# Mean convolutions of a graph network on Trainium2: column halves of the array for alternate tiles, and another spread of a side computation over the two convolutions

## The chip, the core and the metric

The kernel runs on one core of a Trainium2 chip. The core has a matrix engine (TensorE, PE in the profile, with its weight loads shown as PEld), a vector engine (VectorE, DVE), a scalar engine (ScalarE, ACT), a gather and custom engine (GpSimd, POOL) and a queue engine that issues transfers (SyncE, SP). They run side by side, each in its own order, and wait for one another by semaphores. On-chip memory (SBUF) has 128 partitions; products land in the accumulators (PSUM), 128 partitions too.

The metric is the device time of one execution in microseconds (us), less is better. It takes in the whole network, of which the change touches one stage.

## The reference

The network has 3125 nodes with 64 features and 100000 edges, sorted by destination. Four blocks stand one after the other, each on h = max(layernorm(x), 0), and each adds its result to x: a stack of three transformer convolutions, a tensor-field convolution, two mean convolutions, and two relational convolutions over 65 edge types. The change is in the third block:

```
def _sage_conv(x, src, dst, n_nodes, w_l, b, w_r):
    msg = x[src]
    agg = segment_sum(msg, dst, num_segments=n_nodes)
    cnt = segment_sum(ones, dst, num_segments=n_nodes)
    mean = agg / maximum(cnt, 1.0)[:, None]
    return mean @ w_l + b + x @ w_r
...
h = relu(_sage_conv(x, src, dst, n, w1_l, b1, w1_r))
return _sage_conv(h, src, dst, n, w2_l, b2, w2_r)
```

The fourth block needs for each edge one over the number of edges of the same destination and the same relation (the mean inside each relation):

```
seg = dst * r + edge_type
cnt = segment_sum(ones, seg, num_segments=n * r)
mean = agg / maximum(cnt, 1.0)
```

Nothing in this count depends on the features, so the kernel does it beside the mean convolutions.

## The kernel before

**Nodes and adjacency.** Nodes lie on 125 partitions in 25 tiles (NP = 125, NT = 25, D = 64). Earlier, the kernel builds a dense table of edge counts between nodes in DRAM, `adj`; the sum over neighbours is then a product of the features with that table. One tile of the table, `adjr`, has 125 source nodes against all 3136 padded destinations (1568 KB in f32); its pool `sa` has four buffers.

**A mean convolution**, `sage(l, sp, fp, pp, beside)`, lines L1315 to L1353. It loads the weights `wl` and the bias `bb`. It holds seven accumulators `acc`, each of 64 partitions (features) by 448 destinations, and for each of the 25 tiles multiplies the tile's features into all seven (L1328): 175 products, each an f32 matmul, which the trace shows as two records. After that come the nodes' own terms: h is transposed in groups of four tiles (L168 on PE, the copy L169 on ACT, result `hT`), multiplied by the second weight in five groups of five (L1334, accumulator `pn`, which shares its place with the transposes), and the bias is added on DVE (L1335, `own`). The sums are copied to `agg` (L1338, four copies on DVE and three on ACT), multiplied by the first weight (L1342, 25 matmuls in five groups), divided by the count (L1345), added to `own` (L1347), and become the new h (L1349) in the first convolution. In the second they are added to x (L1351), with a layer norm behind (L152 to L160).

**The count beside it**, the generator `relation_counts`, L1045 to L1126, is advanced by `next(beside, None)` in the loop over tiles. Its steps:

1. A setup on DVE of some ten operations (L1052 to L1060).
2. 33 steps for pairs of relations, all on 128x784 f32: a mask (L1068), a forward scan (L1070), a backward scan (L1072) and a predicated copy (L1073) on DVE, and two small copies on ACT (L1074, L1075).
3. A middle section (L1079 to L1107). It sums what crosses partitions with four small matmuls on PE (L1086, L1087, from `rsums`, L1083) and prepares places and corrections on DVE.
4. 22 steps of three units each, 66 in all: a mask (L1112) on DVE, a scaled copy on ACT (L1114, two buffers `ract`), a predicated copy on DVE (L1115).
5. A closing part (L1119 to L1126), which ends with two operations on `wrel`: an addition (L1125) and a reciprocal (L1126).

```
for s in range(NT):
    for _ in range(2 if s % 3 else 1):
        next(beside, None)
    rows = sp.tile([P, AC], F32, name="adjr")
    after_added(dma(rows, adj.rearrange("(p t c) o -> p t (c o)", t=NT, c=AC)[:, s, :]).ins)
    for c in range(ANC):
        PE.matmul(acc[c], lhsT=h[:, s, :], rhs=rows[:NP, c * AW:(c + 1) * AW], start=(s == 0), stop=(s == NT - 1))
```

With this rule a convolution advances the count by 41 steps: the first takes the setup, all 33 pairs, the middle section and 6 of the 22 steps; the second takes the rest in its first ten tiles.

**What sets the order.** The kernel is written as one program; a planner in the framework then orders each engine's instructions by its own costs and dependences. Only the masks L1068 and L1112 are held to program order among themselves. So an instruction can stand on its engine well before or after its place in the source. All transfers named here are issued by SP, in that queue's order.

**Behind the stage** the relational block begins (`Relations`): weights `wr` are loaded, h is copied twice (`hh`, L1387 on DVE, L1388 on ACT), transposed, and multiplied by the relation weights (L1396, in two row halves), copied to `xs` (L1400) and stored. Its sums use `wrel`.

Of the kernel before, what the change touches and what calls it, by code (L numbers as in the profile page):

```python
# [9 lines left out]
F32 = mybir.dt.float32  # L10
# [8 lines left out]
P = 128  # L19
N = 3125  # L20
NP = 125
NT = 25
D = 64
# [16 lines left out]
AC = 3136  # L40
ANC = 7
AW = AC // ANC
# [6 lines left out]
def gnn_stack(ctx: ExitStack, tc: tile.TileContext, a: dict, out: bass.AP):  # L49
    nc = tc.nc  # L50
    V, S, PE, GP = nc.vector, nc.scalar, nc.tensor, nc.gpsimd
# [12 lines left out]
    def dma(dst, src):  # L64
        return nc.sync.dma_start(dst, src)
# [7 lines left out]
    def bcast_rows(ap, parts):  # L73
        n = ap.shape[-1]
        return bass.AP(tensor=ap.tensor, offset=ap.offset, ap=[[0, parts], [1, n]])
# [51 lines left out]
    adj = dram.tile([AROWS * AC, 1], F32, name="adj")  # L127
# [6 lines left out]
    h = node.tile([NP, NT, D], F32, name="h")  # L134
# [12 lines left out]
    def layernorm_relu(lp, t0, t1):  # L147
        n = t1 - t0
        st = lp.tile([NP, 3, n], F32, name="lnst", bufs=2)
        cen = lp.tile([NP, n, D], F32, name="lncen", bufs=2)  # L150
        sq = lp.tile([NP, n, D], F32, name="lnsq", bufs=2)
        V.tensor_reduce(st[:, 0, :], x[:, t0:t1, :], axis=AX.X, op=ALU.add)  # L152
        V.tensor_scalar(st[:, 0, :], st[:, 0, :], 1.0 / D, None, op0=ALU.mult)
        V.tensor_sub(cen, x[:, t0:t1, :], st[:, 0, :].unsqueeze(2).to_broadcast([NP, n, D]))
        S.activation(sq, cen, AF.Square)
        V.tensor_reduce(st[:, 1, :], sq, axis=AX.X, op=ALU.add)
        S.activation(st[:, 2, :], st[:, 1, :], AF.Sqrt, bias=eps, scale=1.0 / D)
        V.reciprocal(st[:, 2, :], st[:, 2, :])
        V.tensor_mul(cen, cen, st[:, 2, :].unsqueeze(2).to_broadcast([NP, n, D]))
        V.tensor_scalar(h[:, t0:t1, :], cen, 0.0, None, op0=ALU.max)  # L160
# [333 lines left out]
    def transposed(pool, pp, src, w, name):  # L494

        t = pool.tile([w, NT, NP], F32, name=name)
        transposed_tiles(pp, t, src, w, 0, NT)
        return t
# [361 lines left out]
    def after_each(ins, those, class_, reason):  # L860
        for st in those:
            tc.add_manual_dep(ins, st.name, mybir.DependencyInfo(class_, mybir.DependencyReason.DATA), reason=reason)

    def after_added(ins):
        after_each(ins, added, mybir.DependencyClass.Sync, "sums into the same places")
# [159 lines left out]
    with tc.tile_pool(name="fl", bufs=1) as fp, tc.tile_pool(name="flp", bufs=1, space=PSUM) as pp:  # L1025
# [7 lines left out]
        ps = pp.tile([1, 1], F32, name="ps")  # L1033
# [279 lines left out]


    def sage(l, sp, fp, pp, beside):  # L1315
        wl = fp.tile([D, 2, D], F32, name="wl")
        bb = fp.tile([NP, D], F32, name="bb")
        dma(wl[:, 0, :], a[f"L2_gnn_w{l}_l"])
        dma(wl[:, 1, :], a[f"L2_gnn_w{l}_r"])
        dma(bb, bcast_rows(a[f"L2_gnn_b{l}"], NP))  # L1320
        acc = [pp.tile([D, AW], F32, name=f"acc{c}") for c in range(ANC)]
        for s in range(NT):
            for _ in range(2 if s % 3 else 1):
                next(beside, None)
            rows = sp.tile([P, AC], F32, name="adjr")
            after_added(dma(rows, adj.rearrange("(p t c) o -> p t (c o)", t=NT, c=AC)[:, s, :]).ins)
            for c in range(ANC):
                PE.matmul(acc[c], lhsT=h[:, s, :], rhs=rows[:NP, c * AW:(c + 1) * AW], start=(s == 0), stop=(s == NT - 1))  # L1328
        own = fp.tile([NP, NT, D], F32, name="own")
        hT = transposed(fp, pp, h, D, "hT")  # L1330
        for t0 in range(0, NT, 5):
            ps = pp.tile([NP, 5, D], F32, name="pn", tag="ptr")
            for i in range(5):
                PE.matmul(ps[:, i, :], lhsT=hT[:, t0 + i, :], rhs=wl[:, 1, :], start=True, stop=True)  # L1334
            V.tensor_add(own[:, t0:t0 + 5, :], ps, bb.unsqueeze(1).to_broadcast([NP, 5, D]))  # L1335
        agg = fp.tile([D, AC], F32, name="agg")
        for c in range(ANC):
            (S.copy if c % 2 else V.tensor_copy)(agg[:, c * AW:(c + 1) * AW], acc[c])  # L1338
        for c, t0 in enumerate(range(0, NT, 5)):
            ps = pp.tile([NP, 5, D], F32, name=f"acc{c}")  # L1340
            for i in range(5):
                PE.matmul(ps[:, i, :], lhsT=agg[:, t0 + i:N:NT], rhs=wl[:, 0, :], start=True, stop=True)  # L1342
            o = own[:, t0:t0 + 5, :]
            m = fp.tile([NP, 5, D], F32, name="mean", bufs=2)
            V.tensor_mul(m, ps, rcnt[:, t0:t0 + 5].unsqueeze(2).to_broadcast([NP, 5, D]))  # L1345
            ht = h[:, t0:t0 + 5, :]
            V.tensor_add(m, o, m)  # L1347
            if l == 1:
                V.tensor_scalar(ht, m, 0.0, None, op0=ALU.max)  # L1349
            else:  # L1350
                V.tensor_add(x[:, t0:t0 + 5, :], x[:, t0:t0 + 5, :], m)  # L1351
                layernorm_relu(fp, t0, t0 + 5)

    with tc.tile_pool(name="rc", bufs=1) as rc, tc.tile_pool(name="sa", bufs=4) as sa, tc.tile_pool(
        name="sg", bufs=1
    ) as sg, tc.tile_pool(name="sgp", bufs=1, space=PSUM) as sgp:
        counting = relation_counts(rc, rc, sgp)
        sage(1, sa, sg, sgp, counting)
        sage(2, sa, sg, sgp, counting)
        for _ in counting:  # L1360
            pass
# [111 lines left out]
```

## Time and profile before

| | us |
|---|---|
| runs | 9271.43, 9261.91, 9268.46; median 9268.46 |
| profiled execution: its own time | 9271.42 |
| profiled execution: span on the profile | 9269.6 |
| the stage of the change, first count operation to first `hh` copy | 6367.4 to 6788.9 (421.5) |
| last h of the first convolution (L1349) ends | 6623.2 |
| products of the second convolution (L1328) end | 6742.2 |
| busy in 6367 to 6789: DVE, PE, ACT | 340.3, 328.7, 94.7 |

The page gives for each engine its busy time over the span. Since the blocks have different limits, the stage is read by itself. A timeline row of PE gathers neighbouring records of one kind: start, the time from the first start to the last end, and their number. A waits row names the waiting instruction and line, what released it, the total, how often, and the longest. In a tile's row stand the duration's minimum, median and maximum in ns and the first and last start in us.

### The profile page before, as it was taken

The numbers are of one execution on the slowest core, as the hardware profiler recorded it, in microseconds if no ns is written. First come the engines' busy times: TensorE is split into PE (matmuls) and PEld (weight loads), VectorE is DVE, ScalarE is ACT, GpSimd is POOL, SyncE is SP. The second block draws the span as 40 slices with busy tenths as digits, with TensorE's granted clock in tenths as the row PEclk, the third lists the DMA queues.
The fourth block names the chain that finished last, engine by engine and source line by source line (L and its number), as shares of the span: only waits on it lengthen the run. The fifth ranks groups of instructions, "written<-read, shape, count | busy, mean of one in ns | idle before, by whom it ended". The sixth has DMA issues, their size and how long they took to land. (4 is left out here: it accounts for less than half of the span.)

```text
span 9269.6 us, 70976 instructions
## 1 busy us (share of the span) xinstructions
PE 4731.1 (51%) x20300; PEld 3046.4 (33%) x20300; DVE 5564.9 (60%) x14292; ACT 992.4 (11%) x2654; POOL 6373.5 (69%) x5765
## 2 busy tenths in 40 slices
PE   5555545556455554888788788886770000320000
PEld 3333333333233333555555555552340000110000
DVE  7777766877677774666666666667842222322222
ACT  1111111111111111000000000001320000110000
POOL 3777767777677776888888888881006777447776
PEclk8555555555555556888888888887785555665555
DMA  5665636555355553444444444445463221442221
GB/s 181 205 204 192 204 123 206 198 175 176 114 172 178 174 174 97 108 107 104 112 111 104 112 105 111 103 99 183 171 205 81 52 53 51 127 152 53 51 53 47
DMA packets 677528, 1211.18 MB, mean 131 GB/s; under 512 B 323106, under 2 KB 468024, under 8 KB 633241
## 3 DMA queue, kind: packets, MB, share of 16 engines
q1 hardware_dynamic: 399586, 938.00, 29.3%
q0 software_dynamic: 277536, 268.52, 14.7%
q8 instruction: 163, 2.67, 0.1%
q14 instruction: 243, 1.98, 0.1%
HBM read 670.19 MB, written 535.54 MB: 130 GB/s over the span
## 5 line engine op out<-in xcount | busy, mean ns | idle before, releaser
L68 POOL DMA_INDIRECT kvg<-kvtd,srci x2352 | 2375.1, 1010 | 718.1 <-issue 681.7
L68 POOL DMA_INDIRECT msg<-xw,msgi x1568 | 1502.3, 958 | 1320.9 <-DMA xw<-xs 652.8
L1236 PE MATMUL pa<-cc,zT 128*128 128x256 f32 x6272 | 1623.7, 416 | 0.0
L876 POOL DMA_INDIRECT adj<-adjv,adji x784 | 1247.9, 1592 | 255.2 <-issue 236.8
L1236 PEld LDWEIGHTS pa<-cc,zT 128*128 128x128 f32 x6272 | 1265.5, 207 | 295.8 <-issue 116.9
L68 POOL DMA_INDIRECT xg<-xtf,srci x784 | 928.5, 1184 | 238.9 <-issue 199.5
L674 PE MATMUL pv<-msg,prevm 128*128 128x64 f32 x4 | 1.4, 442 | 2032.1 <-DVE msg L669 2032.1
L1225 DVE TENSOR_TENSOR zT<-xT,pb 128x512 f32<-128x512 f32 x980 | 611.3, 681 | 686.3 <-PE pb L1222 500.2
L78 DVE SCALAR_TENSOR_TENSOR msg<-msg,wrel 128x1024 f32<-128x1024 f32 x98 | 120.1, 1225 | 1390.7 <-DMA msg<-xw,msgi 1390.7
L509 DVE SCALAR_TENSOR_TENSOR data<-data,same 128x66 f32<-128x66 f32 (+2 forms) x3136 | 933.9, 298 | 27.7 <-DVE srest L81 0.3
L932 PE MATMUL pe<-we,eaT 128*128 128x256 f32 x1176 | 557.9, 634 | 768.5 <-DVE kvg L934 708.2
L509 DVE SCALAR_TENSOR_TENSOR qg<-qg,same 128x64 f32<-128x64 f32 (+1 forms) x2940 | 864.9, 294 | 40.8 <-DMA qg<-qtd,dsti 11.4
L934 DVE TENSOR_TENSOR kvg<-kvg,pe 128x1024 f32<-128x1024 f32 x294 | 358.5, 1219 | 691.7 <-DMA kvg<-kvtd,srci 612.6
L674 PEld LDWEIGHTS pv<-msg,prevm 128*128 128x128 f32 x4 | 1.0, 312 | 2033.5 <-issue 1018.3
L932 PEld LDWEIGHTS pe<-we,eaT 128*128 128x128 f32 x1176 | 337.9, 312 | 942.3 <-DVE kvg L934 780.6
L845 DVE SCALAR_TENSOR_TENSOR atie<-pk,akey,amuch 128x512 f32<-128x512 f32 x784 | 579.5, 739 | 43.1 <-PE pk L840 42.7
L840 PE MATMUL pk<-aplace,adig 128*128 128x128 bf16 x2352 | 298.6, 303 | 570.1 <-DVE atie L845 554.3
L840 PEld LDWEIGHTS <-adig 128*128 128x128 bf16 x2352 | 224.2, 138 | 782.3 <-DVE atie L845 432.0
L669 DVE SCALAR_TENSOR_TENSOR msg<-msg,same 128x64 f32<-128x64 f32 x1566 | 446.3, 285 | 56.1
L1210 PE MATMUL px<-ident,xg 128*128 128x128 f32 x784 | 204.9, 346 | 516.9 <-DMA xg<-xtf,srci 491.7
L788 PE MATMUL pw<-w,hid 64*128 64x128 f32 x3136 | 435.5, 410 | 22.2 <-ACT hid L748 22.2
L788 PEld LDWEIGHTS pw<-w,hid 64*128 64x128 f32 x3136 | 366.0, 294 | 124.8 <-issue 79.5
(316 smaller groups left out, 6426.5 us busy)
## 6 DMA issues: line engine op xcount, KB each, us to landing
wt<-wo SPq DMA_DIRECT2D x98, 1024.0 KB
kvg<-wt SPq DMA_DIRECT2D x49, 2048.0 KB
xw<-xs SPq DMA_DIRECT2D x50, 1820.0 KB
adjr<-adj SPq DMA_DIRECT2D x50, 1568.0 KB
qg<-qx SPq DMA_DIRECT2D x144, 512.0 KB
cum_tf<-data SPq DMA_DIRECT2D x49, 1152.0 KB
cum_dt<-data SPq DMA_DIRECT2D x98, 544.0 KB
qxf<-zeros SPq DMA_DIRECT2D x98, 512.0 KB
```

The costliest lines, as they stand in the source:

```text
L68: return GP.indirect_dma_start(out=dst, out_offset=None, in_=table, in_offset=bass.IndirectOffsetOnAxis(ap=idx, axis=0),)
L509: V.scalar_tensor_tensor(t[:, j], t[:, j - 1], same[:, s:s + 1], t[:, j], op0=ALU.mult, op1=ALU.add)
L669: V.scalar_tensor_tensor(m[:, j, :], prev, same[:, g * G + j:g * G + j + 1], m[:, j, :], op0=ALU.mult, op1=ALU.add)
L788: PE.matmul(pw[m][:, i, k, :], lhsT=hid[r, k, i0 + i, :], rhs=w2[r, :], start=False, stop=(i == 1 and k == 1))
L840: PE.matmul(ps[:, i, :], lhsT=dig[:, k, 4 * q + i:4 * q + i + 1].to_broadcast([P, P]), rhs=place[:, k, :], start=(k == 0), stop=(k == 2))
L845: V.scalar_tensor_tensor(t, ps, key[:, s:s + 1], much[:, i], op0=ALU.is_equal, op1=ALU.mult, accum_out=adjv[:, s:s + 1])
L876: st = GP.indirect_dma_start(out=adj[:], out_offset=bass.IndirectOffsetOnAxis(ap=adji[:, s:s + 1], axis=0), in_=adjv[:, s:s + 1], in_offse ...
L932: PE.matmul(pe[:, i], lhsT=eaT[:, 2 * b + i, :], rhs=entry.we, start=True, stop=True)
L934: V.tensor_add(kve, kve, pe.rearrange("p i j d -> p (i j) d").unsqueeze(2).to_broadcast([P, 8, 2, D]))
L1210: PE.transpose(px[:, i, :], cur.xg[:, j0 + i, :], ident)
L1225: V.tensor_mul(zc, xT, pb)
L1236: PE.matmul(pa[t - 1][i // 2][:, i % 2, :], lhsT=z[t - 1][c][:, i, :], rhs=cc[:, c, :], start=(c == 0 and i % 2 == 0), stop=False)
```

## The change

Two things are changed in `sage`.

The products of even tiles go to the accumulators' partitions 0 to 63 and those of odd tiles to partitions 64 to 127, that is to the two column halves of the array, and tiles are taken two at a time with the two products of an accumulator next to each other in the source. The accumulators and `agg` thus have 128 partitions, which hold two partial sums. The first weight is loaded twice, into both halves, so that the mean matmul contracts over 128 partitions and adds the two partial sums.

The count is advanced by one step a tile in the first convolution, and by one or two in the second: 25 steps (the setup and 24 pairs) in the first, up to 34 (9 pairs, the middle section, the 22 steps and the closing part) in the second.

```diff
     def sage(l, sp, fp, pp, beside):
-        wl = fp.tile([D, 2, D], F32, name="wl")
+        wl = fp.tile([2 * D, 2, D], F32, name="wl")
         bb = fp.tile([NP, D], F32, name="bb")
-        dma(wl[:, 0, :], a[f"L2_gnn_w{l}_l"])
-        dma(wl[:, 1, :], a[f"L2_gnn_w{l}_r"])
+        for k in range(2):
+            dma(wl[k * D:(k + 1) * D, 0, :], a[f"L2_gnn_w{l}_l"])
+        dma(wl[:D, 1, :], a[f"L2_gnn_w{l}_r"])
         dma(bb, bcast_rows(a[f"L2_gnn_b{l}"], NP))
-        acc = [pp.tile([D, AW], F32, name=f"acc{c}") for c in range(ANC)]
-        for s in range(NT):
-            for _ in range(2 if s % 3 else 1):
-                next(beside, None)
-            rows = sp.tile([P, AC], F32, name="adjr")
-            after_added(dma(rows, adj.rearrange("(p t c) o -> p t (c o)", t=NT, c=AC)[:, s, :]).ins)
+
+        acc = [pp.tile([2 * D, AW], F32, name=f"acc{c}") for c in range(ANC)]
+        for s0 in range(0, NT, 2):
+            two = range(s0, min(s0 + 2, NT))
+            rows = {}
+            for s in two:
+                for _ in range(2 if l == 2 and s % 3 == 0 else 1):
+                    next(beside, None)
+                rows[s] = sp.tile([P, AC], F32, name="adjr")
+                after_added(dma(rows[s], adj.rearrange("(p t c) o -> p t (c o)", t=NT, c=AC)[:, s, :]).ins)
             for c in range(ANC):
-                PE.matmul(acc[c], lhsT=h[:, s, :], rhs=rows[:NP, c * AW:(c + 1) * AW], start=(s == 0), stop=(s == NT - 1))
+                for s in two:
+                    PE.matmul(acc[c][(s - s0) * D:(s - s0 + 1) * D], lhsT=h[:, s, :],
+                              rhs=rows[s][:NP, c * AW:(c + 1) * AW], start=(s < 2), stop=(s >= NT - 2))
...
-                PE.matmul(ps[:, i, :], lhsT=hT[:, t0 + i, :], rhs=wl[:, 1, :], start=True, stop=True)
+                PE.matmul(ps[:, i, :], lhsT=hT[:, t0 + i, :], rhs=wl[:D, 1, :], start=True, stop=True)
...
-        agg = fp.tile([D, AC], F32, name="agg")
+        agg = fp.tile([2 * D, AC], F32, name="agg")
```

In the order that the planner makes of the changed kernel, the transposes of the first convolution and 22 of its 25 own matmuls stand ahead of its products on PE, where they stood behind them before. The line numbers of the changed kernel are up to seven higher from here on (products L1334, own matmul L1341, own addition L1342, `agg` copies L1345, mean matmul L1349, mean L1352 and L1354, h L1356, x L1358, `hh` L1394 and L1395, relation matmul L1403).

## The prediction

> **What bounds the kernel now.** I read the busy rows of the page, then the mean-convolution stage by stretches, then its waits, then the timeline rows of what ends last there. The page's row for PE shows no engine near full over the program, so the stage (6367 to 6789 us) has to be read by itself. In stretches the columns are busy time of PE, PEld, DVE, ACT, POOL (x instructions), granted clock, DMA share, GB/s.
>
> ```profile
> PE 4731.1 (51%) x20300; PEld 3046.4 (33%) x20300; DVE 5564.9 (60%) x14292; ACT 992.4 (11%) x2654; POOL 6373.5 (69%) x5765
> ```
> ```profile
> 6370.00:6420.00 50.00, 46.09 (x119) 16.78 (x120) 47.74 (x37) 3.06 (x16) 0.00 (x0) 0.93 0.91 351
> ...
> 6520.00:6570.00 50.00, 2.66 (x10) 2.08 (x11) 47.34 (x42) 3.06 (x16) 0.00 (x0) 0.50 0.00 0
> ...
> 6650.00:6700.00 50.00, 50.00 (x135) 18.24 (x134) 46.11 (x58) 29.72 (x30) 0.00 (x0) 1.00 0.86 313
> 6700.00:6745.00 45.00, 44.75 (x127) 17.31 (x125) 22.64 (x24) 10.20 (x12) 0.00 (x0) 1.00 0.50 180
> 6745.00:6790.00 45.00, 27.82 (x115) 24.28 (x115) 19.90 (x58) 7.65 (x18) 0.00 (x0) 0.51 0.00 0
> ```
> DVE is full to 6570 while PE and the DMA stop at about 6501; then PE is full to 6742 and DVE thins out. The stage has two bounds, one after the other. The waits say why PE stops:
>
> ```profile
> PE pc L1086 <- DVE rsums L1083: 66.2, 1, 66.2
> DVE agg L1338 <- PE acc L1328: 21.0, 6, 16.3
> DVE own L1335 <- PE pn L1334: 30.9, 10, 13.6
> ```
> The relation count's small matmul (L1086) stands in PE's order with 8 products of convolution 1 behind it, and its operand exists only after all 33 relation pairs: 66.2 us idle. The other two are DVE waiting for PE at the ends of the convolutions. Durations that I use (minimum/median/maximum ns; then start, length):
>
> ```profile
> L1328 PE MATMUL acc<-adjr,h x700: 538/539/1010, 6373.9 to 6741.6; 125*64 125x448 f32 x175
> L1068 DVE SCALAR_TENSOR_TENSOR rmask<-rhalf,runit x33: 974/975/976, 6371.4 to 6559.2; 128x784 f32<-128x784 f32 x33
> L1112 DVE TENSOR_SCALAR rmask<-runit x66: 550/569/569, 6575.8 to 6713.6; 128x784 f32<-128x784 f32 x66
> ```
> ```profile
> 6613.43 128.75 PE L1328 MATMUL acc<-adjr,h 125*64 125x448 f32 x342
> ...
> 6622.85 0.32 DVE L1349 TENSOR_SCALAR h<-mean 125x320 f32<-125x320 f32 x1
> ...
> 6716.40 5.05 DVE L1126 RECIPROCAL wrel<-wrel 128x784 f32<-128x784 f32 x1
> ...
> 6742.98 1.58 PE L1342 MATMUL acc<-wl,agg 64*125 64x64 f32 x6 [0.25 <-DVE agg L1338]
> 6744.49 0.62 PE L168 MATMUL ptr<-ident,h 125*64 125x125 f32 x4
> ...
> 6826.67 2.84 PE L1396 MATMUL pm<-wr,hT 64*125 64x512 f32 x11
> ```
> A pair of relations comes every (6559.2-6371.4)/32 = 5.87 us, one of the 66 placing units (mask, ACT activation, predicated copy) every 1.74 us. A record of a product lasts 539 ns, but 342 of them take 128.75 us: 0.376 us each, 0.753 a product (two records).
>
> **The change, part by part.** The planner's order of the changed kernel decides more than the diff, so I follow it on each engine.
>
> *Halves.* Tiles s and s+1 go to column halves 0 and 1. In PE's order they do not alternate strictly: for four tiles it has 7 in half 0, 7 in half 1, 4 and 4, then only three pairs in turn. If only neighbours of different halves overlap, 56 record times become about 46. No row shows column halves at once. Ends: row halves (L1396) run at 2.84/11 = 0.258 us a record of 512 columns against 0.376x512/448 = 0.43 alone, so an overlapped pair would save up to 40% of it; at the other end nothing pipelines and each record costs its 0.539. I take 0.376x46/56 = 0.31 us a record, from the L1396 row, the nearest: halves of the same array under f32 records of similar length.
>
> Passages between groups of different shape cost little in the trace: the six L1342 records end at 6742.98+1.58 = 6744.56 and the L168 group behind them starts at 6744.49. With 0.1 us each, some 30 passages a convolution are 3 us, which I count at nothing in convolution 1 (hidden) and hold to be inside the 10 us that I give the transposes of convolution 2. The Trainium skill, "TensorEngine Tiling (Array Packing)", Key Properties, speaks against the change: a change of tiling mode drains the array. By it each passage would pay its last record's unhidden 0.539-0.376 = 0.16 us, 5 us in all; the trace does not bear out more.
>
> *Convolution 1: 24 pairs instead of 33, no middle section.* The 25 transposes and 22 own matmuls now stand ahead of the products on PE. DVE: start 6367.4; setup 4.0 (6367.4 to 6371.4); five own additions 5x0.49 = 2.5 and some 6.5 of waiting for cold own matmuls (they came 2.94 us apart before); 24x5.87 = 140.8. That is 6521 (6367.4+4.0+2.5+6.5+140.8). PE's products, from about 6382, end at 6382+350x0.31 = 6490, without any overlap (0.376) at 6514: hidden either way behind DVE. So are the fourth small weight load and the DMA (25 x 1.606 MB at 426 GB/s, its best rate here, is 94 us). Aggregate copies 2.3, 25 mean matmuls at 0.255x2 = 12.8, last mean, addition and maximum 1.4: 6537.5. Before, the last h ended at 6623.2: 86 us earlier. The 128-row aggregate I price like 64 rows (0.61 us): DVE's 128x784 operation takes 0.57, so partitions are not what costs.
>
> *SP.* The three small weight loads of convolution 2 stand behind its third tile load and wait for the last mean of convolution 1 (about 6535); the 22 tile loads behind them start then. A tile at 426 GB/s takes 3.8 us, seven products at least 4.3, and three tiles (13 us) are already there: hidden, unless PE gets faster than the DMA. The clearing of cum_r that now goes ahead of the wr loads is one more issue among those 5 us.
>
> *Convolution 2: the rest of counting.* DVE: 9x5.87 = 52.8, to 6590; middle section about 9.0 without the copies in it (6565.1 to 6575.8 before), to 6599.5. The wait on L1086 is not gone but halved: after 59 products PE stands from about 6560 to rsums at 6593, some 33 us, 116 products queued behind it. After it PE paces: ACT's copies of hT stand among the activations of the placing units, so a late transpose holds ACT, and ACT holds DVE's predicated copies. PE does 39 products (39x0.62 = 24), with the seven groups of transposes and ACT copies between them (about 1.4 each, the groups alone taking 0.6 to 1.0: 10) and the middle section's own copy and the first own group (about 6): first own addition 6633. Then 28 more products (17) and four own groups (2 each): the fifth at 6658. Alone, DVE would be there at about 6637. Then 21 units x 1.74 = 36.6: 6694.5, when the last 49 products are done (6688); copies and first mean group 7.8: 6702.3. Then 22 units interleaved with small operations (1.39 each, as at 6613 to 6623 before), 30.6, and 16.5 of means and layer norm: 6749.4; L1125 0.97 and the reciprocal 5.05, which ran under PE's products before and now stands ahead of the first hh copy: hh at 6755.4. Before: 6788.9 (L1387), so 33.4 earlier. The first relation matmul came 6.05 after hh, released by its weight load (wr, issued on SP when the counting and product buffers come free). In the changed order the last of them is read by L1125, 5 us ahead of hh, so the load lands in time and only the transpose and its copy remain, 3.4: another 2.6.
>
> Sum: convolution 1 ends 85.7 earlier; from there to hh it takes 6755.4-6537.5 = 217.9 instead of 6788.9-6623.2 = 165.7, 52.2 longer; -85.7+52.2-2.6 = -36, rounded. Everything later (node table, gathers) starts from this point and is the same code. The profiled execution took 9271.4 us, 3.0 above the median of the runs shown: 9271.4-36.0 = 9235.4, or 9232 on the median.
>
> **Rivals.**
> (B) DVE alone paces convolution 2: the hT copies come in time, so the fifth own addition is at 6637, and of those 21 us 17 reach the end (PE's last products hold the rest): gain 53, 9215. For it: ACT is busy only 95 of 421 us in this stage. Against: PE has 67 products to do between the middle section and that addition, which at 0.62 are 42 us. It decides if overlapped records come at half time (0.19), which gives 67x0.38 = 25 us. The Trainium skill, "TensorE: Matmul & The Clock Gate", Part 3 (measured speedup), has three column tiles 2.38 times faster; by it halves in strict alternation would come near this case, and no row here shows columns at once.
> (C) The split orders are kept but the halves run one after the other, each change of half paying the unhidden part of a record, 0.539-0.376 = 0.16 us. About 63 changes of half a convolution: 10 us. In convolution 1 hidden up to 6521; in convolution 2 the 116 late products pay 0.376 for 0.31 (+4 on the path after the middle section) and 7 for changes: gain 25, 9243. This is "the change does not do what it says".
> (D) Slower: records into half an array do not pipeline, 0.539 each. Products of convolution 1 end at 6382+350x0.539 = 6571 instead of hiding under 6521, +50; the late 232 records of convolution 2 take 125 instead of 80, +40 to +45. Total 54 slower, 9322. It decides from 0.45 us a record: 350x(r-0.397)+232x(r-0.376) = 36. Against it: L1396 pipelines in halves; for it: no row shows this shape.
> (E) Same: the moved tail (25 units, the reciprocal) waits 18 us or more beyond my sum, for example if the transposes of convolution 2 come behind 14 products each with late adjr tiles, whose loads stand on SP behind weights that wait for convolution 1's means: 9250 to 9287.
>
> **How the numbers follow.** Forecast 0.47, B 0.19, C 0.14, E 0.08, D 0.12. 0.2% (18.5 us) is about what a measurement here can tell from no change: faster 0.80, same 0.08, slower 0.12. The range, 9204 to 9256, spans from B with a further 11 us (the 33 us stall shorter) to C with a further 13; D and E are left out.
>
> **What would show it.** DVE's 24th pair ending near 6521 with PE done before it; last h of convolution 1 near 6538; one wait on the relation sums of some 33 us at 6560; own additions of convolution 2 waiting for PE up to 6658; the reciprocal directly before the hh copy near 6755. Product records spaced above 0.45 us, or hh later than 6770, would make the prediction wrong.

## The result and the profile after

The changed kernel takes 9227.25 us (median of six runs, 9221.26 to 9234.68) against 9261.86 for the kernel before (six runs, 9259.08 to 9271.43): 34.6 us less, a ratio of 0.9961 with a 95% interval of 0.9950 to 0.9972. The prediction was 9232, the range 9204 to 9256.

The profiled execution of the changed kernel took 9234.68 us (span 9232.9), 36.7 less than that of the kernel before. That is not all the stage's doing: its first count operation (L1052) starts at 6350.87 instead of 6367.39, 16.5 us earlier, though nothing ahead of it was changed. In the thirteen profiles other than that of the last experiment, which came from a slower chip, the stage starts anywhere from 6341 to 6371. So the stage is read from its own start, to the first relation matmul: 6794.91 - 6367.39 = 427.5 before and 6744.29 - 6350.87 = 393.4 after, 34.1 us less. What comes behind the stage is 13.9 us longer in this profile (2488.6 us instead of 2474.7), so its 36.7 us are 16.5 + 34.1 - 13.9. Of these only the 34.1 are shown to come from the change; the other two scatter from profile to profile.

First, the changed kernel by stretches (busy time of PE, PEld, DVE, ACT, POOL, clock, DMA share, GB/s):

```profile
6370.00:6420.00 50.00, 49.02 (x188) 19.82 (x187) 45.44 (x34) 3.06 (x16) 0.00 (x0) 1.00 0.89 357
...
6520.00:6570.00 50.00, 33.54 (x119) 12.84 (x118) 47.56 (x38) 3.06 (x16) 0.00 (x0) 0.81 0.72 290
...
6650.00:6700.00 50.00, 30.77 (x120) 18.82 (x116) 46.31 (x70) 28.59 (x32) 0.00 (x0) 0.72 0.24 97
6700.00:6745.00 45.00, 2.79 (x9) 1.90 (x10) 42.03 (x78) 20.96 (x30) 0.00 (x0) 0.50 0.19 25
```

Before, 6520 to 6570 had 2.66 us of PE and no transfer; it now has 33.54 us and 290 GB/s, because convolution 2 has begun. From 6700 on PE is nearly idle and DVE full, where before PE was full to 6742 and DVE half idle: the placing units have moved to the end. The waits of the stage:

```profile
PE pc L1086 <- DVE rsums L1083: 23.0, 1, 23.0
...
DVE own L1342 <- PE pn L1341: 18.6, 8, 5.7
...
DVE mean L1352 <- PE acc L1349: 8.8, 6, 2.8
DVE link L1115 <- ACT ract L1114: 8.6, 2, 6.1
```

PE still stands before the relation sums, 23.0 us instead of 66.2, and waits 40.5 us at the end of convolution 1 (the row of L1349 below) for the aggregate copies, which stand behind DVE's 24 pairs. DVE waits for PE in the own terms. The products by tile, and PE's and DVE's rows that mark the steps:

```profile
L1334 PE MATMUL acc<-adjr,h x700: 538/539/1009, 6364.7 to 6668.8; 125*64 125x448 f32 x175
```
```profile
6393.94 14.67 PE L1334 MATMUL acc<-adjr,h 125*64 125x448 f32 x56 [0.55 <-DMA adjr<-adj]
...
6508.17 11.90 PE L1349 MATMUL acc<-wl,agg 128*125 128x64 f32 x50 [40.54 <-DVE agg L1345]
...
6587.68 9.29 PE L1334 MATMUL acc<-adjr,h 125*64 125x448 f32 x28
...
6614.35 10.69 PE L1334 MATMUL acc<-adjr,h 125*64 125x448 f32 x28
```
```profile
6350.87 0.57 DVE L1052 CAST rti<-typf 128x784 int32<-128x784 f32 x1
...
6521.27 0.33 DVE L1356 TENSOR_SCALAR h<-mean 125x320 f32<-125x320 f32 x1
...
6643.45 0.49 DVE L1342 TENSOR_TENSOR own<-pn,bb 125x320 f32<-125x320 f32 x1 [4.44 <-PE pn L1341]
...
6736.19 5.05 DVE L1126 RECIPROCAL wrel<-wrel 128x784 f32<-128x784 f32 x1
6741.16 0.43 DVE L1394 COPY hh<-h 125x256 f32<-125x256 f32 x2
```

A record still lasts 539 ns, but in convolution 1 56 of them take 14.67 us (0.262 each, and each such group waits for its tile: PE now outruns the transfers), in convolution 2 groups of 28 take 9.29 (0.332) to 10.69 (0.382, with a granted clock of 0.87 in that stretch and 1.00 in the other), where one half alone took 0.376. The reciprocal stands directly before the hh copy.

The view that decides the rest of this study is a single stretch from the first count operation to the first hh copy, of the kernel before and of the changed one:

```profile
6367.39:6788.86 421.47, 328.70 (x958) 148.35 (x958) 340.66 (x381) 94.66 (x162) 0.00 (x0) 0.82 0.51 191
```
```profile
6350.87:6741.16 390.29, 255.13 (x934) 124.08 (x934) 336.27 (x381) 90.87 (x159) 0.00 (x0) 0.77 0.53 208
```

DVE is busy for 340.7 of 421.5 us and then for 336.3 of 390.3. (The 4 us of difference are overlap of neighbouring operations: the durations of DVE's operations add up to 349.5 us before and 350.1 after.) The stage is DVE's work plus the time in which DVE has nothing to do: 80.8 us before, 54.0 after. PE's busy time fell by 74 us, of which the stage shows little.

### The profile page after: what moved, and what is told of

Same layout as the page of the kernel before. It is cut to its first block, busy times and chain, and to the rows that moved or that the text cites. A ratio compares the mean times of both kernels' runs of the same rounds, so it can differ in the third digit from the quotient of the medians.

```text
span 9232.9 us, 70987 instructions
## 1 busy us (share of the span) xinstructions
PE 4680.0 (51%) x20300; PEld 3030.0 (33%) x20300; DVE 5563.0 (60%) x14292; ACT 990.9 (11%) x2654; POOL 6360.7 (69%) x5765
## 5 line engine op out<-in xcount | busy, mean ns | idle before, releaser
L78 DVE SCALAR_TENSOR_TENSOR msg<-msg,wrel 128x1024 f32<-128x1024 f32 x98 | 120.1, 1225 | 1393.3 <-DMA msg<-xw,msgi 1393.3
```

## The experiments

Times are medians against the kernel before on the same chip, run beside it; "stage" is from the first count operation to the first relation matmul in the run's profile (427.5 before, 393.4 changed), and DVE's idle time is the stretch to the first hh copy less DVE's busy time in it. "The layer's stretch" is from the relation layer's first copy to `xs` (L1400 before, L1407 in the changed kernel) to the first gather from the stored table.

### The count alone

```diff
-            for _ in range(2 if s % 3 else 1):
+            for _ in range(2 if l == 2 and s % 3 == 0 else 1):
```
The edit is made in the kernel before.

> The kernel before with the new rule for the count alone; products in one column half as before. Theory (what the prediction says: convolution 1 is paced by DVE's 24 relation pairs, the products are hidden there with or without halves): last h of convolution 1 some 171 us after the stage's first count operation, as in the changed kernel (before: 256). In convolution 2 the own terms stand at the end of PE's order, so the placing units run without waiting for PE; 121 products at 0.753 us after the sums end some 91 us later, still ahead of DVE. Stage 375 to 385 us against 421.5 before and 390 with both parts: 9217 to 9227. Rival (the halves make the gain): less than 10 us gained, 9252 or more.

9223.0 against 9251.4: ratio 0.9963 (0.9949 to 0.9977). Stage 391.2. Without any column half the stage is as short as with both parts. Convolution 1 ends 167.9 us after the start (expected 171; 170.7 in the changed kernel), although its products run in one half:

```profile
6371.40 134.36 PE L1328 MATMUL acc<-adjr,h 125*64 125x448 f32 x350
...
6580.49 0.64 PE L1086 MATMUL pc<-rsums,prevm 128*128 128x33 f32 x2 [14.30 <-DVE rsums L1083]
...
6582.34 92.42 PE L1328 MATMUL acc<-adjr,h 125*64 125x448 f32 x242
```

134.36 us of products, ending at 6505.8, hide behind DVE's pairs, whose last ends at about the same time. In convolution 2 the 121 products behind the sums take 92.4 us and end at 317, but DVE has placing units to do until 365, and the planner's order of this kernel leaves the own terms to the end, so that no unit waits for them. The stage was expected 6 to 16 us shorter than this; which of DVE's waits the expectation had left out was not worked out.

### The halves alone

```diff
-                for _ in range(2 if l == 2 and s % 3 == 0 else 1):
+                for _ in range(2 if s % 3 else 1):
```
The edit is made in the changed kernel.

> The changed kernel with the old rule for the count. Theory: convolution 1 still carries all 33 pairs on DVE, its last h stays near 255 us after the stage's start, so nothing is gained there; in convolution 2 the products take about 100 us instead of 131 and the layer norm comes without placing units in between: stage 370 to 385, 9215 to 9230. Rival 1 (only the count matters, the halves do nothing anywhere): stage near 421, 9255 to 9265. Rival 2 (halves make the gain in both convolutions): last h of convolution 1 well below 230.

9218.0 against 9251.4: 0.9962 (0.9948 to 0.9975). Stage 391.0, longer than the expected 370 to 385. Convolution 1 ends at 247.3 (before: 255.8), so the halves gain 8 us there, where the theory had nothing; in convolution 2 the products start at 231 and end at 353, and the layer norm comes without placing units between. Both rivals fall: the halves do something, and 28 of the 36.5 us are gained in convolution 2.

So each part alone gives what both give together: 36.3, 36.5 and 34.1 us of the stage. DVE's row says why. The stretch for the count alone and for the halves alone:

```profile
6357.60:6742.90 385.30, 324.37 (x934) 146.90 (x934) 340.17 (x381) 91.05 (x157) 0.00 (x0) 0.85 0.56 209
```
```profile
6340.90:6725.90 385.00, 257.34 (x958) 124.31 (x958) 339.56 (x380) 93.58 (x162) 0.00 (x0) 0.78 0.52 209
```

The same 340 us of DVE's work, and 45 us of idle time instead of 81, in both. Where the idle time went, the last 80 us ahead of the first hh copy on DVE show: the kernel before, the count alone, the halves alone, and both.

```profile
6708.86:6788.86 80.00, 63.10 (x214) 37.78 (x212) 33.82 (x70) 11.77 (x23) 0.00 (x0) 0.73 0.19 70
```
```profile
6662.88:6742.88 80.00, 41.89 (x157) 29.98 (x155) 63.38 (x110) 31.74 (x43) 0.00 (x0) 0.61 0.00 0
```
```profile
6645.91:6725.91 80.00, 57.96 (x215) 29.19 (x213) 70.90 (x114) 33.66 (x41) 0.00 (x0) 0.82 0.50 203
```
```profile
6661.16:6741.16 80.00, 20.08 (x82) 14.82 (x80) 77.00 (x130) 41.68 (x50) 0.00 (x0) 0.57 0.07 15
```

Before, DVE had nothing to do for 46.2 of these 80 us; then for 16.6, 9.1 and 3.0. Either edit alone takes most of that time away, the count by moving work there, the halves by ending the products sooner, so the second edit finds little left. With both, DVE's idle time in the stage is even a little more than with one: it now waits in the middle of convolution 2, some 12 us for the own terms and 9 for ACT's scaled copies.

### Alternating halves, first try

```diff
-                    PE.matmul(acc[c][(s - s0) * D:(s - s0 + 1) * D], lhsT=h[:, s, :], ...
+                    mm = PE.matmul(acc[c][(s - s0) * D:(s - s0 + 1) * D], lhsT=h[:, s, :], ...
+                    if s > s0:
+                        tc.keep_in_program_order(mm)
```

> The changed kernel with each product of the odd tile held directly behind that of the even tile in PE's order, so that the halves alternate strictly. Theory: a pair of records then starts every 0.376 us (0.19 a record; the changed kernel has 0.26 to 0.33), convolution 1 stays paced by DVE (no change there), and DVE's waits for PE in convolution 2 (some 21 us) shrink to about 8: stage 375 to 380, 9212 to 9217. Rival (the overlap is already as good as the DMA lets it be, or each change of half costs a drain): records no closer than 0.26, 9225 to 9235.

9224.6 against 9251.4: 0.9969 (0.9957 to 0.9981), stage 395.3. This run says nothing on alternation: the hold puts an instruction behind the one that the source has before it on its engine, so each odd tile's product stood behind its even tile's, as it had already, and the planner's order (seven products of one half, then seven of the other) stayed. The expectation's premise was wrong, not the theory. Compared with the changed kernel it shows how far two profiles of the same order differ: 2 us.

### Alternating halves

```diff
+                    if c or s > s0:
+                        tc.keep_in_program_order(mm)
```

> The changed kernel with all products of a pair of tiles held in the order of the source, so that the halves do alternate one by one (the run before only held the odd tile's product behind the even tile's, which left the order as it was). Theory (halves overlap when neighbours differ): two records every 0.376 us, 0.19 a record where the data is there, against 0.33 in the changed kernel behind the relation sums; the own additions of convolution 2 come some 15 us earlier, the first relation matmul 380 to 386 us after the stage's start (changed kernel 393). Rival (halves do not overlap more than they do, or DVE's work is the floor already): 390 to 394.

9206.7 against 9252.4: 0.9948 (0.9933 to 0.9963). Stage 382.1, inside the expected 380 to 386. PE's rows of a pair of tiles, one in convolution 1 and one in convolution 2:

```profile
6398.21 5.48 PE L1334 MATMUL acc<-adjr,h 125*64 125x448 f32 x28 [1.04 <-DMA adjr<-adj]
...
6631.12 5.48 PE L1334 MATMUL acc<-adjr,h 125*64 125x448 f32 x28
```

0.196 us a record: two halves of the array take two records in about the time of one (0.376), and nothing is lost at the changes of half. In convolution 1 PE then waits for tiles and little is gained (its last h comes at 169.2 instead of 170.7); in convolution 2 the fifth own addition comes at 276.0 instead of 292.6 and DVE's idle time falls from 54.0 to 42.6 us (378.9 less 336.28 in the row):

```profile
6355.20:6734.10 378.90, 225.43 (x934) 104.51 (x934) 336.28 (x381) 91.01 (x159) 0.00 (x0) 0.73 0.54 214
```

### PE without its stand before the sums

```diff
-            PE.matmul(pc[:, 0, k, :], lhsT=prevm, rhs=sums[:, k, 0, :], start=True, stop=True)
-            PE.matmul(pc[:, 1, k, :], lhsT=prevt, rhs=sums[:, k, 1, :], start=True, stop=True)
+            PE.matmul(pc[:, 0, k, :], lhsT=prevm, rhs=same[:, :RH], start=True, stop=True)
+            PE.matmul(pc[:, 1, k, :], lhsT=prevt, rhs=same[:, :RH], start=True, stop=True)
```

> The changed kernel in which the four small matmuls of the middle section read a tile that is there from the start instead of the sums over relation pairs; what crosses partitions in the count is left out, the operations stay. PE then does not stand at them. Theory: the 23 us for which PE stood in convolution 2 are what makes it late for the own terms and the activations; without them DVE's waits in convolution 2 (21 us) go down to 5 or less and the stage to 370 to 375: 9208 to 9213. Rival (DVE's own work sets the pace and the wait is hidden): stage 385 to 391, 9222 to 9228.

The kernel leaves out what crosses partitions in the count. 9216.2 against 9251.4: 0.9954 (0.9940 to 0.9967). Stage 381.7: 11.7 us less, where 18 to 23 were expected. So about half of the stand of 23 us cost time, in the order that the planner then made (the four matmuls and convolution 2's own terms moved ahead too). DVE's idle time is 42.3 us, as with strict alternation, by another way:

```profile
DVE own L1342 <- PE pn L1341: 18.6, 10, 3.9
```

The own additions moved ahead, beside the relation pairs, and still wait as long in sum; what went are the units' waits for ACT.

### The end of the count beside the relation layer

The count is advanced one step a tile in both convolutions; the last 21 units and the closing part are taken up by the loop over the relation layer's tiles.

```diff
-                for _ in range(2 if l == 2 and s % 3 == 0 else 1):
+                for _ in range(1):
...
+                rel = Relations(0, fp, rw, pp)
+                for t0, t1 in CHUNKS:
+                    rel.tiles(t0, t1)
+                    next(counting, None)
+                for _ in counting:
+                    pass
```

> The changed kernel with the count advanced by one step a tile in both convolutions, so that the last 21 placing units and the closing part (L1119 to L1126) are left over; they are advanced beside the first relation layer's tiles, one step behind each group of tiles, with the pools opened so that both fit. Theory (the stage is DVE's work plus its waits; the work left over is 21x1.74+6 = 43 us): first relation matmul at 350 to 358 us after the stage's start instead of 393, and the relation layer, which stores as it goes, hides most of the 43: 9185 to 9205. Rival (DVE is needed there too, or PE becomes the bound of convolution 2): the stage still shortens, but the time from there to the end grows by as much: 9215 to 9230.

9203.9 against 9252.4: 0.9946 (0.9932 to 0.9959). Stage 355.6, as expected: DVE's work there fell from 336.3 to 301.2 us and the stage by 37.8. But only a part of it reached the end: the layer's stretch took 210.0 us instead of 192.7 in the changed kernel, which takes 17 of the 38 us back, and by the medians this run is 48.5 us ahead of the kernel before, the changed kernel 34.6. Both theories had a part of it right.

```profile
6362.70:6712.20 349.50, 248.11 (x904) 117.78 (x902) 301.16 (x336) 74.03 (x143) 0.00 (x0) 0.81 0.53 208
```

### Both of these

> The two edits before together: strict alternation and the left-over steps beside the relation layer. Theory: with fewer placing units PE's own pace counts more in convolution 2, so alternation is worth 5 to 10 us here: first relation matmul at 342 to 352 us, 9178 to 9197. Rival (alternation is worth nothing where DVE sets the pace): within 3 us of the run without it.

9200.9 against 9252.4: 0.9942 (0.9928 to 0.9956); stage 343.8, 11.8 us less than without alternation. In the stage alternation is worth the same here as there (11.3); by the medians the two runs differ by 3 us alone, and their intervals overlap. The total is above the expected 9178 to 9197; the layer's stretch is 211.6 us.

### The masks on POOL

```diff
-            tc.keep_in_program_order(V.tensor_scalar(m, place, float(u), None, op0=ALU.is_equal))
+            tc.keep_in_program_order(GP.tensor_scalar(m, place, float(u), None, op0=ALU.is_equal))
```

> The changed kernel with the 66 masks of the placing units (L1112) made by POOL, which is idle in this stage, instead of DVE: 66x0.67 = 44 us of DVE's pace taken away if POOL keeps up. Theory (DVE's work is the floor): DVE's busy time in the stage falls by 37 us and the stage by 15 to 25, since PE then is late in convolution 2 and the layer norm stays: first relation matmul at 368 to 378 us. Rival (POOL takes longer than 1.07 us for a mask, so that the copies wait for it, or the two engines hinder each other): no gain or a loss of up to 60 us.

9290.1 against 9252.4: ratio 1.0045 (1.0029 to 1.0060), slower by 38 us, stage 463.9. The rival holds. POOL's mask and DVE's wait for it:

```profile
L1112 POOL TENSOR_SCALAR rmask<-runit x66: 2166/2167/2802, 6579.7 to 6798.2; 128x784 f32<-128x784 f32 x66
```
```profile
DVE link L1115 <- POOL rmask L1112: 121.2, 65, 2.3
```

DVE's work did fall (310.6 us), but POOL takes 2.17 us for what DVE does in 0.57. The mask has one buffer, so POOL begins the next one only when DVE's copy has read the last: a unit comes every 3.36 us ((6798.2-6579.7)/65), where it was 1.74. What a second buffer would give was not run; POOL's 2.17 alone is above 1.74. Less work on the bounding engine shortens the stage only if what replaces it is quicker than its pace.

### The end of the count behind the layer's tiles

```diff
                 for t0, t1 in CHUNKS:
                     rel.tiles(t0, t1)
-                    next(counting, None)
                 for _ in counting:
                     pass
```
The edit is made in the kernel with both of the edits above.

> Strict alternation and the left-over 21 units, but these are advanced behind all tiles of the relation layer instead of between them (with strict alternation alone and the units between, the stretch from the layer's first copy to its first gather took 212 us instead of 190, and DVE then waited 21 us for the first gathered data). Theory (the units hold up the layer's copies to xs, which its stores wait for): that stretch comes down to 190 to 197 and the units run while DVE waits for the gather: 9178 to 9190. Rival (the layer is slower for another reason, such as its transfers): the stretch stays above 205 and the time near 9200.

9215.3 against 9266.6: 0.9946 (0.9932 to 0.9959), no gain on the run before it. The layer's stretch stayed at 214.7 us; the stage is 344.4. This could not yet separate the two: the planner had put the units among the last 20 of DVE's 100 copies to xs all the same.

### The sums later

Ten empty steps are put between the sums and their matmuls, which are held behind the products of 14 tiles, and the count's steps are shifted (two in each of the first five tiles of convolution 2).

```diff
+        for _ in range(10):
+            yield
         pc = pp.tile([P, 2, 2, RH], F32, name="pc", tag="ptr")
...
-                for _ in range(1):
+                for _ in range(1 if l == 1 or 5 <= s < 14 else 2 if s < 5 or s % 2 else 1):
```

> The same with the four matmuls of the middle section issued behind the products of 14 tiles of convolution 2 instead of 8.7, and the count's steps shifted so that its DVE work stays in the same places. Theory (PE's stand before the sums, 24.6 us with strict alternation, is what still makes it late in convolution 2): the stand falls to 5 us or less, DVE's waits for PE too, and the relation layer's first copy comes 6 to 12 us earlier than without: 9168 to 9184. Rival (PE now holds DVE at the sums, or the wait was hidden): no gain, within 3 us.

9205.3 against 9266.6: 0.9935 (0.9922 to 0.9949). Stage 339.7 against 344.4: 4.7 us, less than the 6 to 12 expected. PE no longer waits for the sums at all, it comes to them 2.4 us late instead, and the next transposes wait 5.9 us for the copy of the result:

```profile
6590.75 0.41 PE L1088 MATMUL pc<-rsums,prevm 128*128 128x33 f32 x2
...
6598.59 1.04 PE L168 MATMUL ptr<-ident,h 125*64 125x125 f32 x4 [5.87 <-DVE rcin L1091]
```

### One half, with the end of the count behind the layer

> The left-over units behind the relation layer's tiles, but with the products in one column half as in the kernel before. What do halves bring once DVE has 43 us less to do? Theory: in convolution 2 PE becomes the bound, 112 products behind the sums at 0.753 us take 84 us instead of some 55, and the planner leaves the own terms behind the means: the layer's first copy comes 20 to 35 us later than with strict alternation (338 us after the stage's start, so 358 to 373). Rival (halves are worth nothing here either): within 5 us of 338.

The edit is made in the kernel before: one step of the count a tile, and its end behind the layer's tiles as two runs before. 9245.9 against 9266.6: 0.9979 (0.9970 to 0.9988). Stage 382.6 against 344.4 with alternating halves: with DVE's work cut, the products in one half cost 38 us. The first copy to xs comes at 384.7, later than the expected 358 to 373; part of it is the own terms, which the planner again leaves to the end (the last own addition at 363.2, with alternation 269.0), so the 38 us are not the products' alone.

### The end of the count held behind the layer's copies

```diff
+                with tc.issue_after(rel.last[0]), tc.issue_after(rel.last[1]):
                     for _ in counting:
                         pass
```
`rel.last` are the layer's last copies to xs on DVE and on ACT; the edit is made in the kernel with the sums later.

> The run with the sums later, and the left-over units and the whole closing part held behind the last copies to xs on DVE and on ACT (in the two runs before, the planner had put most of them ahead of the last tiles' copies after all). Theory (units among the copies hold up the layer's stores): the stretch from the layer's first copy to its first gather comes down from 214 to 188 to 197 us, the closing part (L1121 to L1126 here, 5 us) leaves the stage as well, and the units run in the wait for the first gathered data, of which some 5 to 10 us are too short: 9170 to 9190 with before at 9255 to 9267. Rival (the layer is slower for its transfers, or the units now hold up the first multiplication L78 by as much): the stretch above 205, or the first L78 no earlier than 575 us after the stage's start: 9200 or more.

This run came on another chip, on which the kernel before takes 10515.6 us, so only the ratio and the stretches inside the profile are compared: 0.9913 (0.9900 to 0.9927). The layer's stretch is 195.2 us instead of 214.0, as the theory had it; the stage 335.3. The first multiplication with the reciprocals (L78) comes at 562.4 instead of 577.2, and it waits for the gathered data, not for the count:

```profile
7914.04 5.05 DVE L1128 RECIPROCAL wrel<-wrel 128x784 f32<-128x784 f32 x1
7920.76 1.23 DVE L78 SCALAR_TENSOR_TENSOR msg<-msg,wrel 128x1024 f32<-128x1024 f32 x1 [1.67 <-DMA msg<-xw,msgi]
```

The units among the copies were what held up the layer. DVE's first 80 copies to xs took 145.8 us in the changed kernel and its last 20 took 29.4. With the units between all tiles it was 160.0 and 31.7, with the units among the last 20 copies 147.1 and 52.0, and here 143.8 and 32.7.

The first gather comes 23.2 us earlier than in the run with the sums later, the first multiplication only 14.8. Of the 8.4 us between, 5.7 are in the first sixteen issues of the gathers on POOL, two of which stand here: the first beside DVE's placing units, the second beside the reciprocal.

```profile
7898.48 1.43 POOL L68 DMA_INDIRECT msg<-xw,msgi  x1 [0.30 <-issue]
...
7914.09 0.94 POOL L68 DMA_INDIRECT msg<-xw,msgi  x1 [0.30 <-issue]
```

Eleven of the sixteen take 1.42 to 1.43 us here; in the run with the sums later, with no unit beside them, all sixteen take 0.94 to 0.97. So the units still cost something where they now stand.

This version beats both kernels; how many microseconds it gains on the first chip was not measured.

## Why the prediction was right, and where its steps were off

The sign, the place and the size were right: 34.6 us by the medians and 34.1 in the stage, where 36 were forecast. The steps of the stage came out close. Counted from the first count operation, predicted and measured:

| step | predicted | measured |
|---|---|---|
| 24th pair ends | 153.6 | 155.1 |
| convolution 1's products end | 123 | 116.8 |
| last h of convolution 1 | 170.1 | 170.7 |
| PE's stand before the sums | 33 | 23.0 |
| first own addition of convolution 2 | 265.6 | 263.6 |
| fifth own addition | 290.6 | 292.6 |
| first aggregate copy of convolution 2 | 327.1 | 329.4 |
| first hh copy | 388.0 | 390.3 |
| first relation matmul | 391.4 | 393.4 |

**Convolution 1 is DVE's.** Right, and shown: its end does not move when the halves are taken away (167.9) or made strict (169.2).

**"56 record times become about 46."** The term was mis-sized. In convolution 1 56 records took 14.67 us, 39 record times of 0.376, and that with tiles arriving at the transfers' pace; behind the sums it was 0.332 to 0.382 a record against my 0.31. The rule that only neighbours of different halves overlap is too narrow: in an order of seven and seven it would give 46 record times. In convolution 1 DVE hides the error. From the sums to the first own addition it took 38.0 us where 40 were forecast, and from there to the fifth 29.0 where 25 were: errors of both signs, so that the sum of these two came out near is in part luck. Strict alternation gave 0.196, nearly the full factor of two.

**The stand before the sums.** 33 predicted, 23.0 measured: PE reached it later, at 203 us instead of 193. The 193 (6560) does not come out of the prediction's own terms: its mean matmuls end at 6536, and 59 products of 0.62 us behind them end at 6573, which leaves a stand of 20. PE did begin these products only behind all the mean matmuls (at 6520.00, 169 us after the start), and its weight loads waited 0.5 us for tiles there. The error reached nothing, since the sums came when forecast. What I did not work out was what the stand costs: removing it gave 11.7 us.

**PE and ACT pace convolution 2 between the sums and the fifth own addition.** Right within 2 us; strict alternation took 11 us of it away. Rival B, DVE's own pace, would have had a stage of 427.5 - 53 = 374.5; that edit and the removed stand go some of the way there (382.1 and 381.7).

**Rivals C and D.** C's premise, halves one after the other with a price for each change, is excluded by the 39 record times for 56 records, and by 0.196 us a record in strict alternation; D's 0.539 a record is excluded by the same rows. (In D the late 232 records are put at 80 us for the forecast; at the forecast's 0.31 they are 72.) E did not occur.

**"Everything later starts from this point and is the same code."** The weak step. The layer's stretch took 185.8 us before and 192.7 after, and 189.5 to 195.4 in the six other runs whose layer was left as it was. So some 4 to 10 us of a stage's gain seem to be given back there. But from the first relation matmul to the end it took 2474.7 us before and 2465.6 to 2478.1 in these six, against 2488.6 in the profile of the changed kernel. With one profile of each kernel it stays open whether anything is lost.

**What the prediction missed** is the attribution. It followed the planner's combined order and so got the sum, but it did not say that the parts overlap in their effect. The sum by parts would have been 73 us of the stage; it is 34, since both take away the same idle time of DVE at the end of convolution 2.

## What to carry to other kernels

Before adding up the gains of two edits, take the busy time of the fullest engine out of the stage: what is left is all that a reordering can win that leaves that engine its work, and two edits that fill the same idle time do not add. Cost the order that the scheduler made, not the order of the source; here the source alternated the halves and the instructions did not, and holding them to it was worth another 11 us of the stage. When a stage is down to one engine's work, look for a later stretch in which that engine waits and the result is not yet needed, and see that the work really lands behind what that stretch is waiting for.

## What the runs showed of the hardware that I had not expected

Two column halves run records of 539 ns side by side at nearly full rate: 28 in 5.48 us (0.196 each), against 0.376 each in one half, with no price to be seen for changing half at every product.

With seven products in one half and then seven in the other, 56 records still took 39 record times instead of the 46 that a start in order, with overlap only where the halves change, would give. So products of the later seven start while earlier ones of the first seven have yet to. In the single records of that group four start alone, 0.376 to 0.43 apart, and then ten pairs at once; in the 28 records of 9.29 us ten start alone and then four pairs. What sets how far ahead PE looks the traces do not show.

POOL takes 2.17 us for a compare of 128x784 f32 values that takes DVE 0.57. Its issue of one gather took 1.43 us beside DVE's placing units (a compare and a predicated copy each) and 0.94 beside DVE's reciprocal.
